# First attention of a four-layer sequence model: deeper step order, shared key projection, transposes by VectorE, tiles closed by pairs

## The chip, the cores and the metric

The kernel runs on one core of one Trainium2 chip. The time is the device time of one execution in microseconds (us). The core has five engines that each work through their own list of instructions: TensorE (PE in the profile; its weight loads are PEld), VectorE (DVE), ScalarE (ACT), GpSimd (POOL) and SyncE (SP). SP only issues transfers (DMAs) here. The engines meet through semaphores. SBUF is the working memory with 128 partitions; PSUM, 8 banks of 128 x 512 float32, takes what TensorE computes. [...]

## The reference

Eight stages follow one another on a sequence of 1024 tokens with 256 features: four times attention and a feed-forward part, each added to its input and followed by a layer normalization. The change is in the first attention and at the seam to the first feed-forward part, a mixture of eight experts of which each token takes two. Cut to what matters:

```python
# first attention: 16 query heads, 4 key/value heads, head size 128, window 64
q, k = rotate(x @ Wq), rotate(x @ Wk); v = x @ Wv
q1, q2 = q[..., :64], q[..., 64:]; k1, k2 = k[..., :64], k[..., 64:]
allowed = (col <= row) & (col >= row - 63)
a1 = softmax(where(allowed, q1 @ k1.T / 8, -inf))
a2 = softmax(where(allowed, q2 @ k2.T / 8, -inf))
diff = relu(a1 - lam[head] * a2)
diff = diff / (diff.sum(-1) + 1e-6)
x = layernorm(x + (diff @ v) @ Wo)

# first feed-forward part
logits = x @ Wr                        # 8 experts
top2, selected = top_k(logits, 2); w = softmax(top2)
out = sum over the two experts of w * ((clip(silu(x @ Wg)) * (x @ Wu)) @ Wd)
x = layernorm(x + out)
```

## The kernel before

The activations x lie in SBUF as eight tiles of 128 tokens (`k.x`), with a transposed copy `k.xT` made by `transpose_two` (two tiles at a time). Each stage is a function; `four_layers` calls them in turn, with a pool of buffers for each kind of tile, whose number stands in `SCOPES`.

**Units.** The first attention, `attn0`, works in 32 units: for each of the four key heads g, eight tiles t of 128 tokens. A unit takes the four query heads of g for its tile, as two pairs r and two blocks b of 64 queries, each with a window of 128 keys. Each head's vector is split into two halves f (first and second softmax).

**Operands.** Keys and queries are projected and rotated by `operands(g, half)` for 512 tokens at once, in steps that are spread over the units before they are needed: `next(ahead)` does one step. A step is a projection into a bank (`project`, L159) and a multiplication by cosine and sine (L627 for queries, L629 for keys, on VectorE); every second step adds the two rotating combinations on GpSimd (L634, L635). There are three pairs of steps per half: one for keys and two for queries. The key weights hold each head's columns twice, so that a key tile carries the same 64 rows in its lower and in its upper partitions, one copy for each pair r of query heads.

**A unit's steps.** `attn0_probs` writes the masks and the scores into two banks (L723, L733), takes the maxima of the eight rows of scores (L741, VectorE) and the exponentials (L749, ScalarE, eight instructions). Its second part makes the factor lam times the ratio of the two sums (L757, L758, L759) and, for each of four blocks, the difference (L765, VectorE) and its positive part with its sum (L769, ScalarE). Its third part takes the reciprocal of the sum (L773, L775) and multiplies by it on GpSimd (L777). `attn0_values` transposes the four blocks on TensorE (L786), copies them from PSUM on ScalarE (L788), multiplies by the values (L792), copies the result (L798), multiplies by the output weights (L804) and adds to x (`add_rows`, L240).

**The order.** `k.in_order()` makes TensorE, ScalarE, VectorE and GpSimd work in the order in which the program writes the instructions. SP is not among them: its order is set by the scheduler of the framework. The loop in `attn0` runs over i. In iteration i it writes, in this order: the transposes of unit i-3; the third part's predecessor for unit i-1 (factor and differences); a step of `operands` (and, for g = 0, the values of one tile, L166, L667); the values of unit i-3; the scores and exponentials of unit i; in odd iterations another step; the third part of unit i-1; the output sums of unit i-3. From scores to sums it is thus three iterations. The buffers limit how far an engine can run ahead: four banks, two double banks ("wide") for scores, three e, four diff, three pt and three ot tiles.

**The seam.** After the loop `k.layernorm()` normalizes four tiles at a time (L209, L210, the root on ScalarE at L227, L213). `ffn0` then stores the normalized rows to `moe_rows` in memory (L838), loads 24 pieces of expert weights (L844, L847), computes the router's logits for all eight tiles (L166), and finds the two largest and their indices (L874 to L880). From L881 to L956 it ranks the choices and builds the table of tokens for each block of an expert; `gather` (L233) then fetches the rows of `moe_rows` in that order.

## Time and profile before

| | us |
|---|---|
| median of three runs | 2273.65 |
| lowest and highest run | 2271.97, 2276.45 |
| the profiled execution | 2268.97 |
| its span, first to last instruction | 2267.1 |
| busy in the span: TensorE | 2073.2 |
| VectorE | 1284.3 |
| ScalarE | 872.9 |
| GpSimd | 528.9 |

The first attention lies in the first 292 us of the span. The last addition of its output (L240) ends at 291.75, and the first gather of the feed-forward part starts at 313.45. Two instructions that it has no use for yet stand later in the profile: VectorE's transposition of 32 x 32 squares (L402) and the transfers pt<-turned (L408), by which the second and the fourth attention transpose their probabilities.

How to read the lines that follow: a line of the busy times by stretch gives the stretch in us from the span's start, its length, then for each engine the busy time and the number of instructions, then the clock that TensorE was granted (1.00 is full), the share of the 16 DMA engines, and GB/s. A line of the groups gives line, engine, operation, output and inputs with their shapes and the count, then the busy time and the mean in ns, then the idle time ahead of them and what ended it. A line of the timeline gives start and duration in us. A line of the transfers gives the issues, the size of one and the median time from issue to landing in us.

### The profile page before, as it was taken

The page shows a single profiled execution, that of the slowest core. Times are in us where ns is not written, and L with a number is a line of the kernel's source. Part 1 is how long each engine was busy: PE and PEld are TensorE (multiplying, and loading weights), DVE is VectorE, ACT ScalarE, POOL GpSimd, SP SyncE. Part 2 cuts the span into 40 slices and gives each one's busy share as a digit, 9 for nine tenths or more (in the row PEclk, how much of TensorE's full clock was granted, in tenths as well). Part 3 has the DMA queues.
Part 4 walks back from the last instruction along what each step waited for, and adds up shares of the span by engine and source line. Part 5 has one row for each costly group of instructions (what it writes and reads, how often), then busy time and mean ns, then how long its engine had stood idle before and what let it go on. Part 6 is the DMA issues. An engine that isn't in the chain of part 4 may idle for free.

```text
span 2267.1 us, 24836 instructions
## 1 busy us (share of the span) xinstructions
PE 2073.2 (91%) x8127; PEld 1221.8 (54%) x8127; DVE 1284.3 (57%) x2599; ACT 872.9 (39%) x2268; POOL 528.9 (23%) x807
## 2 busy tenths in 40 slices
PE   7999769699999998988888998899999988999997
PEld 4666545466666665754444443366666665444443
DVE  5677646577776665455773445267777664222223
ACT  3666624343343433344454222654444442111111
POOL 4333221333333333321111000333333330000000
PEclk9999979799999999999999999999999999999999
DMA  4100054254545544013200000034344340111100
GB/s 161 36 10 29 29 174 117 62 140 112 135 108 132 155 112 100 10 56 111 68 1 10 28 28 2 19 85 110 90 115 90 77 113 19 38 31 53 31 1 19
DMA packets 124255, 159.60 MB, mean 70 GB/s; under 512 B 28928, under 2 KB 96064, under 8 KB 124128
## 3 DMA queue, kind: packets, MB, share of 16 engines
q1 hardware_dynamic: 114544, 132.98, 22.5%
q0 software_dynamic: 9584, 25.05, 3.7%
q8 instruction: 65, 1.06, 0.2%
q14 instruction: 62, 0.51, 0.1%
HBM read 68.72 MB, written 17.17 MB: 38 GB/s over the span
## 4 chain that ended last, share of the span: by engine, by line
PE 70%; DVE 13%; ACT 6%; DMA 4%; issue 3%; POOL 2%; SPq 2%; DVEq 0%; ACTq 0%; POOLq 0%
PE bank L159 23%; PE wide L274 8%; PE bank L439 8%; PE wide L307 8%; PE bank L166 4%; ACT e L749 3%; DMA pt<-turned 3%; DVE turned L402 2%; PE bank L1164 2%; PE bank L815 2%; PE bank L1601 1%; DVE st L741 1%; PE bank L995 1%; PE bank L1339 1%; POOL p L267 1%
## 5 line engine op out<-in xcount | busy, mean ns | idle before, releaser
L159 PE MATMUL bank<-xT,w 128*128 128x512 f32 (+2 forms) x1520 | 659.2, 567 | 4.0 <-DVE xT L185 3.8
L159 PEld LDWEIGHTS bank<-xT,w 128*128 128x128 f32 (+1 forms) x1520 | 288.6, 195 | 272.8 <-issue 251.3
L402 DVE STREAM_TRANSPOSE turned<-p 128x128 f32<-128x128 f32 (+7 forms) x232 | 283.6, 1223 | 84.2 <-DMA pt<-turned 48.2
L274 PE MATMUL wide<-k,q 128*128 128x512 f32 (+3 forms) x768 | 294.3, 493 | 18.4 <-ACT p L259 17.5
L267 POOL TENSOR_SCALAR p<-p,st 128x128 f32<-128x128 f32 (+7 forms) x256 | 190.3, 744 | 484.9 <-DVE st L266 484.3
L439 PE MATMUL bank<-pt,v 128*128 128x256 f32 x1216 | 282.6, 374 | 12.8 <-DMA pt<-turned 12.0
L439 PEld LDWEIGHTS bank<-pt,v 128*128 128x128 f32 x1216 | 227.5, 192 | 66.8 <-issue 24.1
L254 DVE TENSOR_REDUCE st<-wide 128x1 f32<-128x128 f32 (+7 forms) x256 | 193.4, 756 | 51.5 <-PE wide L279 44.4
L274 PEld LDWEIGHTS wide<-k,q 128*128 128x128 f32 x768 | 140.1, 192 | 135.3 <-issue 92.7
L307 PE MATMUL wide<-t,w 128*128 128x512 f32 x392 | 187.6, 601 | 8.2 <-DVE t L1878 4.8
L259 ACT ACTIVATE p<-wide,st,factor 128x128 f32<-128x128 f32 (+7 forms) x128 | 106.3, 830 | 214.0 <-POOL st L256 209.4
L259 ACT ACTIVATE p<-wide,st 128x128 f32<-128x128 f32 (+7 forms) x128 | 94.8, 740 | 237.2 <-DVE st L254 218.7
L2201 DVE TENSOR_TENSOR t<-t,bank 128x512 f32<-128x512 f32 x66 | 45.3, 687 | 247.2 <-PE bank L159 247.2
L2200 ACT ACTIVATE t<-bank 128x512 f32<-128x512 f32 x66 | 39.4, 597 | 294.1 <-PE bank L159 279.7
L307 PEld LDWEIGHTS wide<-t,w 128*128 128x128 f32 x392 | 68.2, 189 | 113.4 <-issue 48.3
L166 PE MATMUL bank<-w,xT 128*128 128x512 f32 (+3 forms) x320 | 123.9, 524 | 1.1 <-DVE st L266 0.8
L249 DVE TENSOR_TENSOR wide<-wide,causal 128x128 f32<-128x128 f32 x192 | 55.9, 291 | 97.7 <-PE wide L274 96.4
L749 ACT ACTIVATE e<-wide,st 128x128 f32<-128x128 f32 x256 | 89.8, 376 | 49.5 <-DVE st L741 34.4
L1626 ACT ACTIVATE pt<-wide 128x1024 f32<-128x1024 f32 (+3 forms) x96 | 75.6, 810 | 70.2 <-PE wide L1620 68.3
L2194 POOL COPY t<-select 99x128 bf16<-99x128 bf16 (+1 forms) x33 | 9.4, 291 | 318.7 <-PE bank L1045 318.7
L166 PEld LDWEIGHTS bank<-w,xT 128*128 128x128 f32 x320 | 58.8, 207 | 46.1 <-issue 39.9
L240 DVE TENSOR_TENSOR x<-bank,x 128x256 f32<-128x256 f32 x120 | 47.9, 409 | 55.5 <-PE bank L804 20.8
(317 smaller groups left out, 2921.3 us busy)
## 6 DMA issues: line engine op xcount, KB each, us to landing
pt<-turned SPq DMA_DIRECT2D x60, 240.0 KB, 4.8
pt<-turned SPq DMA_DIRECT2D x60, 176.0 KB, 3.5
w<-in_L_ffn_gate_up_dram SPq DMA_DIRECT2D x16, 512.0 KB, 3.7
pt<-turned SPq DMA_DIRECT2D x28, 256.0 KB, 4.9
pt<-turned SPq DMA_DIRECT2D x60, 112.0 KB, 2.6
pt<-turned SPq DMA_DIRECT2D x28, 224.0 KB, 4.3
w<-in_L_attn_Wq_dram SPq DMA_DIRECT2D x12, 512.0 KB, 9.7
w<-in_L_attn_Wo_dram SPq DMA_DIRECT2D x12, 512.0 KB, 3.8
```

Source lines behind the costliest of these rows:

```text
L159: self.nc.tensor.matmul(out, lhsT=weight(c), rhs=self.xcols(c, lo, n), start=c == 0, stop=c == NC - 1)
L166: self.nc.tensor.matmul(out, lhsT=self.xcols(c, lo, n), rhs=weight(c), start=c == 0, stop=c == NC - 1)
L249: nc.vector.tensor_tensor(scores[:, n - P : n], scores[:, n - P : n], self.causal, ALU.add)
L254: nc.vector.tensor_reduce(top, scores[:, :n], axis=AX.X, op=ALU.max, negate=True)
L259: nc.scalar.activation(probs[:, :n], scores[:, :n], AF.Exp, bias=top, scale=1.0 if scale is None else scale, accum_out=total,)
L267: self.nc.gpsimd.tensor_scalar(probs[:, :n], probs[:, :n], total, 1.0, ALU.mult, ALU.mult)
L274: self.nc.tensor.matmul(s[:, lo : lo + m], lhsT=query, rhs=key(lo, m), start=True, stop=not masked or lo + m < n, skip_group_check=masked,)
L307: nc.tensor.matmul(acc[m][:, half * HALF : (half + 1) * HALF], lhsT=down[:, m * P : (m + 1) * P], rhs=h, start=i == 0, stop=i == count - 1,)
L402: k.nc.vector.transpose(squares.rearrange("p b (k q) -> p b k q", q=32), probs[:, :n].rearrange("p (k i b) -> p b k i", b=4, i=32),)
L439: self.k.nc.tensor.matmul(out.rearrange("p (a q) -> p a q", q=32) if first else out.rearrange("p (s a q) -> p s a q", s=2, q=32), lhsT=val ...
L749: nc.scalar.activation(e[:, r, f, b, :], sc[:, r, f, b, :], AF.Exp, bias=top[:, at : at + 1], accum_out=total[:, at : at + 1],)
L1626: nc.scalar.activation(two[:, :, lo:], sc[:, :, lo:], AF.Exp)
```

## The change

- **Keys.** The columns of the key weights are no longer doubled; the half vectors of two neighbouring heads g and g+1 (g even) stand in one projection of 128 columns, one head in the lower and one in the upper 64 partitions. `operands` makes keys only for an even g, for both heads. GpSimd writes each head's half into its own tile on 64 partitions (four operations instead of two), and four transfers on SP copy each half into the other 64 partitions. There are six key tiles instead of four.
- **Transposes.** `attn0_turned` transposes 32 x 32 squares of the four blocks on VectorE (128 x 512 in one instruction), and four transfers of 32 partitions each put the squares into place in pt. TensorE's transposes and ScalarE's copy go. The values are multiplied by the same numbers in another arrangement of the free dimension.
- **Order.** In iteration i: the turn of unit i-3; a step of `operands` (and values for g = 0); scores and exponentials of unit i; factor and differences of i-1; the third part of i-2; the multiplication by the values for i-4; in odd iterations another step; the output sums of i-5. The loop has 37 iterations instead of 35.
- **Closing.** When both tiles of a pair have their last sum (g = 3), `close` is started for the pair: statistics, root (by a power on GpSimd, `power`), normalization and a store to `moe_rows`, the transposes, the router's logits with the maxima and indices of the pair, one part at a time, at two places in an iteration. What is left when the loop ends runs after it. `ffn0` finds the choices (`k.chosen`), the differences of logits (`k.prob`) and `k.xT` ready; `k.layernorm()`, the four calls of `transpose_two` ahead of `ffn0` and its router are gone.
- **Routing.** The comparison of columns (L931, 128 x 2048) is done in four parts, each ahead of the four products that use it; the copy of the tokens stands after the experts.

The router's weights `wr` move from the pool of weights to the constants and are loaded at the start. The helpers `add_stats`, `power`, `norm_tile`, `transpose_two` and `project_rows` are not changed.

```diff
--- before.py
+++ after.py
@@ -580,13 +580,7 @@
...
-    load_keys(0)
+    wk = k.weights([P, NC, 512], a["L0_attn_Wk"].rearrange("(c p) f -> p c f", p=P))
...
@@ -631,34 +624,96 @@
             if i == 0:
                 yield
         x, y = parts
-        nc.gpsimd.tensor_tensor(first, x[:, 0], y[:, 1], ALU.subtract)
-        nc.gpsimd.tensor_tensor(second, y[:, 0], x[:, 1], ALU.add)
+        for rows, out in first:
+            nc.gpsimd.tensor_tensor(out, x[rows, 0], y[rows, 1], ALU.subtract)
+        for rows, out in second:
+            nc.gpsimd.tensor_tensor(out, y[rows, 0], x[rows, 1], ALU.add)
         yield
 
...
+        heads = range(g, g + 2) if g % 2 == 0 else ()
         if half == 0:
-            keys[g] = [k.tile("k", [P, PAD + T]) for _ in range(2)]
-            for kt in keys[g]:
-                nc.gpsimd.memset(kt[:, :PAD], 0.0)
-        cols = slice(PAD + half * HALF, PAD + (half + 1) * HALF)
-        yield from rotated(
-            lambda i, c: wk[g // 2][:, c, (g % 2 * 2 + i) * P : (g % 2 * 2 + i + 1) * P],
-            half, *(kt[:, cols].rearrange("p (b n) -> p b n", n=64) for kt in keys[g]), 0.125,
-        )
+            for j in heads:
+                keys[j] = [k.tile("k", [P, PAD + T]) for _ in range(2)]
+                for kt in keys[j]:
+                    nc.gpsimd.memset(kt[:, :PAD], 0.0)
+        if heads:
+            cols = slice(PAD + half * HALF, PAD + (half + 1) * HALF)
+            own = [slice(j * 64, j * 64 + 64) for j in range(2)]
+            yield from rotated(
+                lambda i, c: wk[:, c, (g + i) * P : (g + i + 1) * P], half,
+                *(
+                    [
+                        (own[j], keys[g + j][f][own[j], cols].rearrange("p (b n) -> p b n", n=64))
+                        for j in range(2)
+                    ]
+                    for f in range(2)
+                ),
+                0.125,
+            )
+            for j in range(2):
+                for f in range(2):
+                    kt = keys[g + j][f]
+                    nc.sync.dma_start(out=kt[own[1 - j], cols], in_=kt[own[j], cols])
...
+                half, *([(slice(0, P), q[:, :, pair, :])] for q in queries[g, half]), 1.0,
...
+
+    wr = k.tile("const", [P, NC, 8], tag="wr")
+    nc.sync.dma_start(out=wr, in_=a["L0_ffn_Wr"].rearrange("(c p) e -> p c e", p=P))
+    k.moe_rows = k.tile("dram", [T, D], tag="moe_rows")
+    k.chosen = k.tile("const", [P, 2, NT], tag="chosen")
+    k.prob = k.tile("const", [P, 2, NT], tag="prob")
+
+    def close(t):
+
+
+        stats = k.tile("st", [P, 4, 2], tag="stats", bufs=2)
+        for i in range(2):
+            k.add_stats(t + i, stats)
+        rstd = k.power(stats[:, t % 4 : t % 4 + 2, 1], 2, LN_EPS, tag="root")
+        yield
+        for i in range(2):
+            k.norm_tile(t + i, stats, rstd[:, i : i + 1])
+        nc.sync.dma_start(
+            out=k.moe_rows[t * P : (t + 2) * P, :].rearrange("(t p) d -> p t d", p=P),
+            in_=k.x[:, t : t + 2, :],
+        )
+        yield
+        k.transpose_two(t)
+        yield
+        ps = k.bank()[:, :16].rearrange("p (t e) -> p t e", t=2)
+        for i in range(2):
+            k.project_rows(ps[:, i, :], lambda c: wr[:, c, :], (t + i) * P)
+        logits, top = (k.tile("st", [P, 2, 8]) for _ in range(2))
+        which = k.tile("st", [P, 2, 8], U32)
+        nc.vector.tensor_copy(logits, ps)
+        for i in range(2):
+            nc.vector.max(top[:, i, :], logits[:, i, :])
+            nc.vector.max_index(which[:, i, :], top[:, i, :], logits[:, i, :])
+        for i in range(2):
+            nc.vector.tensor_copy(k.chosen[:, i, t : t + 2], which[:, :, i])
+        nc.vector.tensor_tensor(
+            k.prob[:, 1, t : t + 2], top[:, :, 1], top[:, :, 0], ALU.subtract
+        )
+        yield
+
+    closing = []
+
+    def close_on():
+        if closing and next(closing[0], k) is k:
+            closing.pop(0)
 
...
@@ -679,15 +734,11 @@
         for _ in operands(*runs[0]):
             pass
         units = [(g, t) for g in range(4) for t in range(NT)]
-        ahead, made = iter(()), {}
-        for i in range(len(units) + 3):
-            ending = iter(())
-            if i >= 3:
-                g, t = units[i - 3]
-                ending = attn0_values(k, t, g, made.pop(i - 3), (even, odd), wo[g])
-            next(ending, None)
-            if i - 1 in made:
-                next(made[i - 1])
+        ahead, made, outputs = iter(()), {}, {}
+        for i in range(len(units) + 5):
+
+            if i - 3 in made:
+                made[i - 3] = attn0_turned(k, made[i - 3])
             if i < len(units):
                 g, t = units[i]
                 if t % 4 == 0:
@@ -700,16 +751,26 @@
                 next(ahead, None)
                 if g == 0:
                     make_values(t)
-            next(ending, None)
-            if i < len(units):
                 made[i] = attn0_probs(k, t, g, queries[g, t // 4], keys[g], lam)
                 next(made[i])
-                if i % 2:
-                    next(ahead, None)
+            close_on()
             if i - 1 in made:
-                made[i - 1] = next(made[i - 1])
-            for _ in ending:
+                next(made[i - 1])
+            if i - 2 in made:
+                made[i - 2] = next(made[i - 2])
+            if i - 4 in made:
+                g, t = units[i - 4]
+                outputs[i - 4] = attn0_values(k, t, g, made.pop(i - 4), (even, odd), wo[g])
+                next(outputs[i - 4])
+            if i % 2:
+                next(ahead, None)
+            close_on()
+            for _ in outputs.pop(i - 5, ()):
                 pass
+            if i >= 5 and units[i - 5][0] == 3 and units[i - 5][1] % 2:
+                closing.append(close(units[i - 5][1] - 1))
+        while closing:
+            close_on()
 
 
 def attn0_probs(k, t, g, queries, keys, lam):
@@ -778,21 +839,32 @@
     yield four
 
 
-def attn0_values(k, t, g, four, values, wo):
+def attn0_turned(k, four):
+
+
+
+    turned = k.tile("turned", [P, 4, P])
+    k.nc.vector.transpose(
+        turned.rearrange("p b (k q) -> p b k q", q=32),
+        four.rearrange("p k (i b) -> p b k i", b=4),
+    )
+    pt = k.tile("pt", [P, 4, 2, 2, 32])
+    for at in range(4):
+        k.nc.sync.dma_start(
+            out=pt[:, at].rearrange("p r b q -> p (r b q)"), in_=turned[at * 32 : at * 32 + 32]
+        )
+    return pt
+
+
+def attn0_values(k, t, g, pt, values, wo):
 
     nc = k.nc
-    ps = k.bank()
-    for i in range(4):
-        nc.tensor.transpose(ps[:, i * P : (i + 1) * P], four[:, i, :], k.ident)
-    pt = k.tile("pt", [P, 2, 2, P])
-    nc.scalar.copy(pt.rearrange("p r b n -> p (r b n)"), ps)
-    yield
     out = k.bank()
     for b in range(2):
         nc.tensor.matmul(
-            out[:, b * 256 : (b + 1) * 256].rearrange("p (r n) -> p r n", r=2),
-            lhsT=values[b][t][:, g * P : (g + 1) * P], rhs=pt[:, :, b, :],
-            start=True, stop=True,
+            out[:, b * 256 : (b + 1) * 256].rearrange("p (r a q) -> p r a q", r=2, a=4),
+            lhsT=values[b][t][:, g * P : (g + 1) * P],
+            rhs=pt[:, :, :, b, :].rearrange("p a r q -> p r a q"), start=True, stop=True,
         )
...
@@ -828,17 +900,11 @@
...
-    rows = k.tile("dram", [T, D], tag="moe_rows")
+    rows = k.moe_rows
     results = k.tile("dram", [blocks * P, D], tag="moe_results")
-    wr = k.weights([P, NC, 8], a["L0_ffn_Wr"].rearrange("(c p) e -> p c e", p=P))
...
-    for half in range(2):
-        nc.sync.dma_start(
-            out=rows[half * HALF : (half + 1) * HALF, :].rearrange("(t p) d -> p t d", p=P),
-            in_=k.x[:, 4 * half : 4 * half + 4, :],
-        )
...
@@ -866,21 +932,10 @@
...
-    ps = k.bank()[:, : NT * 8].rearrange("p (t e) -> p t e", t=NT)
-    for t in range(NT):
-        k.project_rows(ps[:, t, :], lambda c: wr[:, c, :], t * P)
-    logits, top = small([P, NT, 8]), small([P, NT, 8])
-    which = small([P, NT, 8], U32)
-    nc.vector.tensor_copy(logits, ps)
-    for t in range(NT):
-        nc.vector.max(top[:, t, :], logits[:, t, :])
-        nc.vector.max_index(which[:, t, :], top[:, t, :], logits[:, t, :])
-    chosen, mine = small([P, 2, NT]), k.tile("route", [P, 2, NT, 8], tag="mine", bufs=1)
-    for i in range(2):
-        nc.vector.tensor_copy(chosen[:, i, :], which[:, :, i])
...
@@ -928,10 +983,6 @@
...
-    nc.vector.tensor_tensor(
-        is_column, cols.unsqueeze(1).to_broadcast([P, 2 * NT, P]),
-        column.unsqueeze(2).to_broadcast([P, 2 * NT, P]), ALU.is_equal,
-    )
...
@@ -946,14 +997,15 @@
...
     for i in range(2 * NT):
+        if i % 4 == 0:
+            nc.vector.tensor_tensor(
+                is_column[:, i : i + 4, :], cols.unsqueeze(1).to_broadcast([P, 4, P]),
+                column[:, i : i + 4].unsqueeze(2).to_broadcast([P, 4, P]), ALU.is_equal,
+            )
         nc.tensor.matmul(
             ps, lhsT=is_column[:, i, :], rhs=is_block[:, i // NT, i % NT],
             start=i == 0, stop=i == 2 * NT - 1,
         )
-    low = small([P, blocks])
-    nc.vector.tensor_copy(low, ps[:, 0, :])
-    tokens = k.tile("route", [P, blocks], I32, tag="tokens", bufs=1)
-    nc.vector.scalar_tensor_tensor(tokens, ps[:, 1, :], float(P), low, ALU.mult, ALU.add)
...
@@ -964,10 +1016,13 @@
...
+    low = small([P, blocks])
+    nc.vector.tensor_copy(low, ps[:, 0, :])
+    tokens = k.tile("route", [P, blocks], I32, tag="tokens", bufs=1)
+    nc.vector.scalar_tensor_tensor(tokens, ps[:, 1, :], float(P), low, ALU.mult, ALU.add)
+
+    prob = k.prob
     p1, p2 = prob[:, 0, :], prob[:, 1, :]
-    nc.vector.tensor_tensor(p2, top[:, :, 1], top[:, :, 0], ALU.subtract)
...
@@ -2207,7 +2262,7 @@
...
-    attn0: dict(wide=2, mask=1, rope=1, k=4, v=16, q=4, t=4, e=3, diff=4, pt=3, ot=3),
+    attn0: dict(wide=2, mask=1, rope=1, k=6, v=16, q=4, t=4, e=3, diff=4, turned=2, pt=3, ot=3),
...
@@ -2226,11 +2281,11 @@
...
-            mine = {attn1: (), ffn1: (), ffn2: (), attn2: (0, 2), ffn3: ()}
+            mine = {ffn0: (), attn1: (), ffn1: (), ffn2: (), attn2: (0, 2), ffn3: ()}
             for t in mine.get(stage, range(0, NT, 2)):
                 k.transpose_two(t)
             stage(k, a)
-            if stage in (attn0, attn1):
+            if stage == attn1:
...
@@ -2256,11 +2311,10 @@
...
-    wk = a["L0_attn_Wk"].reshape(D, 4, 2, 1, 64)
-    a["L0_attn_Wk"] = np.broadcast_to(wk, (D, 4, 2, 2, 64)).reshape(D, 1024)
+    wk = a["L0_attn_Wk"].reshape(D, 2, 2, 2, 64)
+    a["L0_attn_Wk"] = wk.transpose(0, 1, 3, 2, 4).reshape(D, 512)
...
```

## The prediction

> **What bounds the kernel now.** I read the busy time by stage first, cutting at the starts of the score maxima (L741, one per unit: unit 0 at 28.26 us, 8 at 93.15, 28 at 247.44, 31 at 269.58).
>
> ```profile
> core 0: us, PE busy (x) PEld busy (x) DVE busy (x) ACT busy (x) POOL busy (x), PEclk, DMA share, GB/s
> 28.30:93.10 64.80, 60.76 (x308) 36.50 (x308) 44.57 (x95) 42.60 (x211) 22.27 (x21) 1.00 0.15 38
> 93.10:247.40 154.30, 141.86 (x796) 94.32 (x796) 116.27 (x250) 101.84 (x516) 58.31 (x54) 1.00 0.08 26
> 247.40:269.60 22.20, 15.13 (x103) 11.82 (x103) 10.66 (x35) 16.54 (x85) 3.12 (x3) 0.96 0.05 15
> 269.60:291.80 22.20, 15.61 (x63) 11.68 (x64) 9.79 (x36) 8.93 (x32) 3.18 (x8) 0.89 0.16 51
> 291.80:313.50 21.70, 9.50 (x69) 8.88 (x67) 14.10 (x71) 3.07 (x4) 0.05 (x1) 0.58 0.91 288
> ```
>
> In the loop (first two rows) TensorE is busy 92 to 94% at full clock: it is the bound. A unit takes 154.3/20 = 7.72 us. In the third row, with no projections left, no engine is full; the chain of waits there runs maxima, exponentials, copy to pt, values, scores. Row four is the drain, row five normalization and routing up to the first gather. Next the groups of instructions by line, for the second row alone:
>
> ```profile
> L159 PE MATMUL bank<-xT,w 128*128 128x512 f32 x116 | 55.6, 602 | 0.0
> L741 DVE TENSOR_REDUCE st<-wide 128x8 f32<-128x1024 f32 x20 | 24.4, 1221 | 3.0 <-PE wide L733 2.9
> L765 DVE SCALAR_TENSOR_TENSOR diff<-e,st 128x128 f32<-128x128 f32 x80 | 22.8, 347 | 1.4 <-DVE st L759 0.5
> L777 POOL TENSOR_TENSOR diff<-diff,st 128x512 f32<-128x512 f32 x20 | 20.8, 1040 | 27.0 <-DVE st L775 27.0
> L786 PE MATMUL bank<-ident,diff 128*128 128x128 f32 x80 | 12.0, 273 | 0.0
> L758 DVE TENSOR_TENSOR st<-st 128x4 f32<-128x4 f32 x20 | 8.9, 446 | 0.7
> ```
>
> L758 handles four numbers and averages 446 ns, though one alone takes 160. The timeline shows why:
>
> ```profile
> 181.90 1.26 POOL L635 TENSOR_TENSOR q<-t,t 128x512 f32<-128x512 f32 x1
> 181.92 1.26 DVE L758 TENSOR_TENSOR st<-st 128x4 f32<-128x4 f32 x1
> 183.12 1.03 POOL L777 TENSOR_TENSOR diff<-diff,st 128x512 f32<-128x512 f32 x1
> 183.21 0.96 DVE L759 TENSOR_TENSOR st<-st,lam 128x4 f32<-128x4 f32 x1
> ```
>
> Each small VectorE instruction ends just as the GpSimd one beside it ends. VectorE has slack today, so this costs little. Last, what the new instructions cost: the groups by form, first attention's later cousin (L402), and the list of transfers; then routing in the timeline.
>
> ```profile
> L402 DVE STREAM_TRANSPOSE turned<-p 128x512 f32<-128x512 f32 x15 | 16.6, 1110 | 0.2
> ```
> ```profile
> pt<-turned SPq DMA_DIRECT2D x28, 64.0 KB, 2.2
> ```
> ```profile
> 291.33 0.42 DVE L240 TENSOR_TENSOR x<-bank,x 128x256 f32<-128x256 f32 x1 [3.92 <-PE bank L804]
> 301.97 0.23 DVE L874 COPY route<-bank 128x64 f32<-128x64 f32 x1 [2.95 <-PE bank L166]
> 304.42 0.29 DVE L881 TENSOR_TENSOR mine<-cols,route 128x128 f32<-128x128 f32 x1
> 313.45 1.25 POOL L233 DMA_INDIRECT rows<-moe_rows,tokens  x1 [33.29 <-DVE experts L966]
> ```
>
> **What the Trainium skill says.** GPSIMD Engine Reference, Key points: GpSimd shares its SBUF interfaces with VectorE and contends with VectorE instructions that have two SBUF inputs. The trace agrees (1.26 us for L758). L765 has two SBUF inputs as well, but never met GpSimd here. VectorE: DVE Perf Modes, The three transpose paths: VectorE transposes only 32x32 blocks; so the four transfers per unit are needed to move the squares between partitions. TensorE: Matmul & The Clock Gate, Part 1: the clock halves after about 3.4 us of idling; here it is 1.00 in the loop and 0.89 in the drain.
>
> **The change, part by part.** TensorE, back to back: a projection 1.72 us, masks and scores 1.28, values 0.86, output sums 1.71, transposes 0.57. A four-unit stretch with six projections is 28.0 today. Keys of two heads at once leave six projections in the stretches that prepare an even g and four in the others: 8 projections fewer. Without transposes TensorE needs 25.7 or 22.3 per stretch, 6.4 or 5.6 a unit. ScalarE loses L788 (0.61): about 4.8 a unit.
>
> VectorE becomes the bound. Its new order in an iteration is: turn (1.05 from start to next start), rotation (1.13), maxima (1.14), the factors (0.60), four L765 (1.06), norm (0.37), second rotation in odd iterations, add (0.38). Today's trace gives all these steps; the turn is L402's 1.11, less the overlap of about 0.06 that the rotations show. Iteration by iteration:
>
> - One rotation: the turn of unit u follows the norm of u by only an add, and needs L777 of u: 0.17 to start, 1.04, 0.08 back. So VectorE idles: 1.05+1.13+1.14+0.60+1.06+0.37+1.29 = 6.64. Behind the waiting turn stand the next rotation and maxima; ScalarE's exponentials wait for the maxima, and TensorE for the banks that the rotation frees.
> - Two rotations: the second covers L777: 6.9. No rotation: 5.5.
> - A rotation pair that ends in the first rotation sends GpSimd 2 operations (queries, 2x1.27) or 4 (keys: two heads by two parts, each 64 partitions; I price each at 1.27, since its free size is the same). They run while the factors and L765 want SBUF. The maxima cover one; the rest hold VectorE: about 1.2 us for queries, 3.4 for keys, if L765 is held too (2.3 if it is not, 0 to 1 if 64 partitions cost half). I take the dear values, since the skill's sentence covers L765 and today's holds last to the end of each operation; the cheap ones go into rival (a).
>
> Six-projection stretch: 6.64 + (6.9+3.4) + (6.64+1.2) + 6.9 = 31.7. Four-projection stretch: 6.64 + (6.9+1.2) + (6.64+1.2) + 5.5 = 28.1. Today: 31.1 in both.
>
> Units 8 to 28 are three stretches of four projections and two of six: 147.7 against 154.3, **-6.6**.
> Units 0 to 8, today limited by TensorE: two projections fewer (-3.4), five transposes (-2.9), two output sums and one values put off by the depth (-4.3): **-10.6**. VectorE, with few stages filled, needs no more than the 54.2 that are left. The start stays: the key copies come off GpSimd at about 20 us and land by about 23, and the queries release the first scores at 26.28 anyway. They hold the SP queue ahead of weights that are wanted only units later.
> Units 28 to 31: three iterations of 5.5 against 22.1: **-5.6**.
> Drain. From the last maxima: exponentials 2.9, factors and L765 in the next iteration, norm, L777, turn; adding VectorE's steps, with the first pairs' closings among them (statistics 1.4, norms 0.75, copy 0.68, maxima and indices 1.6 a pair), iterations 31 to 34 take 6.0+5.8+3.3 and the last turn 1.05: 16.2. Then 4 issues at 0.6, 2.2 to land, values 0.9, two output sums 3.4 and the add 0.4: 9.3 (the copy to ot goes under the first sum). Together 25.5 against 22.2. Expert weights (256 KB each, 5.4 to 5.9 us to land) stand ahead of the last two units' transfers on SP: +0.7, at most +8. So **+4**.
> After the last add, two of the four pairs of tiles are closed, the third is halfway. Its transposes, rows and maxima take 4.3; the fourth's statistics 1.4, root 0.5, norms 0.8, transposes and copy 1.3, rows 1.6, maxima and indices 1.6: 11.5 to the comparison at L881, today 12.7 from the add's end (304.42-291.75). Splitting the column comparison by fours lets TensorE start early: -0.4 of 9.0. **-1.6**. Gathers wait also for the last moe_rows transfer, which may queue behind 2 MB of weights (about 7 us at 288 GB/s), less than the routing's 8.6.
>
> Other edits cost nothing: wr and the key weights (512 KB less) load early; the roots move from ScalarE to GpSimd, which is idle by then; six k buffers only hold memory. In the loop the 128 transfers of squares take SP 2.4 us an iteration and need 4.6 from the turn, while values come an iteration later: covered by 6 us, and without that cover TensorE would wait up to 4.6 per unit. In the built order, weight loads for the second attention stand between them on SP; those wait for projections or output sums that end before the next turn.
>
> Sum: -6.6-10.6-5.6+4-1.6 = -20.4. The profiled execution took 2268.97 (span 2267.1) and becomes 2248.6; the median of the runs is 4.7 higher: 2273.65-20.4 = **2253**.
>
> **Rivals.** (a) *TensorE stays the bound*: GpSimd's short operations hold nothing, and the turn finds L777 done. Then units 8 to 28 take 3x22.3+2x25.7 = 118.3, not 147.7: 2224, and half of that gain 2238. For it: the hold on L765 was never seen. Against: L758 shows the hold, and the turn follows its norm at once. (b) *The turn eats the loop's gain*: VectorE is also held in the turn, or key operations of 64 partitions are dearer, at 0.5 us a unit: +10, and a drain that meets the weights fully +5: 2268. For it: GpSimd is at work 58 of 154 us. Against: L402 keeps 1110 ns beside GpSimd's L267. (c) *Slower: the clock*. TensorE, now waiting on VectorE up to 3.4 us in key iterations, loses full clock. Units 8 to 28 need 5.9 a unit of TensorE work; the change turns slower once that exceeds 8.4 us, a mean clock below 0.70; at 0.65 it is 9.1 a unit, 2288. For it: 0.89 in the drain. Against: units 28 to 31 ran 0.96 at 68% busy, and the loop would be at 80%.
>
> **How the numbers follow.** Forecast 0.55 (2243 to 2263), (a) 0.17, (b) 0.16, (c) 0.12. The range leaves out most of (c) and the far end of (a): 2232 to 2270. Differences below 0.2% (4.5 us) can't be told from none by such runs: faster takes the forecast, (a) and over half of (b), 0.81; same 0.08; slower 0.11.
>
> **What would show it.** In the changed profile: VectorE at about 90% in units 8 to 28 and TensorE at 80%; idle before the turns put down to GpSimd's multiply (L838), near 0.8 us in half the iterations; L819 and L820 averaging over 500 ns and L826 stretched in key iterations; stretches of about 28 and 32 us; the first gather near 293. The prediction is wrong if TensorE waits for pt, if the clock leaves 1.00 in the loop, or if the turn never waits.

## The result and the profile after

The changed kernel takes 2255.48 us (median of four runs, 2252.74 to 2258.68) where the kernel before took 2272.81 us beside it (2271.30 to 2276.45): ratio 0.9922, 95% interval 0.9909 to 0.9935. The forecast was 2253. The profiled execution has a span of 2253.0 us against 2267.1.

The busy times by stretch, cut where the maxima of units 0, 8, 28 and 31 start (L802, formerly L741) and at the last addition and the first gather (us from the start, length; busy time and count of each engine; TensorE's clock; DMA share; GB/s):

```profile
core 0: us, PE busy (x) PEld busy (x) DVE busy (x) ACT busy (x) POOL busy (x), PEclk, DMA share, GB/s
28.40:85.20 56.80, 53.60 (x257) 31.08 (x258) 43.73 (x90) 36.73 (x195) 21.26 (x18) 0.94 0.41 99
85.20:230.20 145.00, 129.20 (x693) 85.99 (x691) 127.03 (x265) 90.64 (x500) 56.16 (x52) 0.95 0.26 63
230.20:246.40 16.20, 12.88 (x90) 9.54 (x90) 12.99 (x38) 13.59 (x76) 3.12 (x3) 1.00 0.23 51
246.40:276.00 29.60, 22.61 (x93) 18.41 (x92) 20.20 (x75) 8.39 (x38) 6.37 (x12) 0.83 0.63 183
276.00:296.20 20.20, 6.25 (x48) 4.72 (x46) 13.32 (x64) 1.49 (x2) 0.71 (x2) 0.56 0.57 181
```

The loop's main part (second row) went from 154.3 to 145.0 us; VectorE is busy 88% of it. The drain (fourth row) went from 22.2 to 29.6 us, at a clock of 0.83. The first gather comes at 296.18 us instead of 313.45: 17.3 us, as much as the medians differ.

Groups of the changed kernel in that second row (busy us, mean ns of one, idle time before and who ended it):

```profile
L826 DVE SCALAR_TENSOR_TENSOR diff<-e,st 128x128 f32<-128x128 f32 x80 | 27.1, 400 | 0.7
L847 DVE STREAM_TRANSPOSE turned<-diff 128x512 f32<-128x512 f32 x20 | 22.0, 1102 | 10.8 <-POOL diff L838 10.8
L820 DVE TENSOR_TENSOR st<-st,lam 128x4 f32<-128x4 f32 x20 | 12.3, 616 | 0.7
L628 POOL TENSOR_TENSOR k<-t,t 64x512 f32<-64x512 f32 x4 | 5.0, 1262 | 4.9 <-DVE t L622 4.7
```

The turn costs 1102 ns, and VectorE stands still ahead of it for 10.8 us in 12 of 20 units until GpSimd's multiplication (L838) is done. GpSimd's operations on 64 partitions take 1262 ns, as long as those on 128. The timeline of one pair of key steps shows what they hold:

```profile
151.42 2.60 POOL L628 TENSOR_TENSOR k<-t,t 64x512 f32<-64x512 f32 x2 [2.35 <-DVE t L622]
152.78 1.26 DVE L820 TENSOR_TENSOR st<-st,lam 128x4 f32<-128x4 f32 x1
154.08 3.27 DVE L826 SCALAR_TENSOR_TENSOR diff<-e,st 128x128 f32<-128x128 f32 x4
154.08 2.60 POOL L630 TENSOR_TENSOR k<-t,t 64x512 f32<-64x512 f32 x2
```

L820, 0.16 us alone, takes 1.26; the four L826, 1.14 us together elsewhere, take 3.27: 3.2 us per key pair, where the prediction's dear value was 3.4.

### The profile page after: what moved, and what is told of

Its sections match the earlier page's. It is cut to its first block, busy times and chain, and to the rows that moved or that the text cites. A ratio compares the mean times of both kernels' runs of the same rounds, so it can differ in the third digit from the quotient of the medians.

```text
span 2253.0 us, 24727 instructions
## 1 busy us (share of the span) xinstructions
PE 2060.1 (91%) x7967; PEld 1211.3 (54%) x7967; DVE 1306.5 (58%) x2640; ACT 851.0 (38%) x2232; POOL 532.1 (24%) x811
## 3 DMA queue, kind: packets, MB, share of 16 engines
q8 instruction: 64, 1.05, 0.2%
## 4 chain that ended last, share of the span: by engine, by line
PE 66%; DVE 9%; ACT 3%; DMA 3%; issue 3%; POOL 2%; SPq 1%; DVEq 0%; ACTq 0%; POOLq 0%
PE bank L159 22%; PE wide L274 9%; PE bank L439 8%; PE wide L307 8%; PE bank L166 4%; DVE turned L402 2%; PE bank L1219 2%; DMA pt<-turned 2%; PE bank L887 2%; PE bank L1656 2%; PE bank L1394 1%; PE bank L1050 1%; ACT pt L1681 1%; PE wide L1669 1%; POOL p L267 1%
## 5 line engine op out<-in xcount | busy, mean ns | idle before, releaser
L159 PE MATMUL bank<-xT,w 128*128 128x512 f32 (+1 forms) x1488 | 644.9, 567 | 6.3 <-DVE xT L185 6.0
L159 PEld LDWEIGHTS bank<-xT,w 128*128 128x128 f32 x1488 | 286.5, 196 | 272.9 <-issue 248.0
L166 PE MATMUL bank<-w,xT 128*128 128x512 f32 (+2 forms) x288 | 118.6, 549 | 0.8 <-DVE st L266 0.8
L249 DVE TENSOR_TENSOR wide<-wide,causal 128x128 f32<-128x128 f32 x192 | 55.8, 291 | 97.1 <-PE wide L274 96.0
L166 PEld LDWEIGHTS bank<-w,xT 128*128 128x128 f32 x288 | 52.6, 196 | 46.2 <-issue 40.0
L1633 DVE TENSOR_REDUCE st<-wide 128x2 f32<-128x1024 f32 x64 | 64.3, 1020 | 21.2 <-PE wide L1629 10.3
```

The source lines that it names most:

```text
L159: self.nc.tensor.matmul(out, lhsT=weight(c), rhs=self.xcols(c, lo, n), start=c == 0, stop=c == NC - 1)
L166: self.nc.tensor.matmul(out, lhsT=self.xcols(c, lo, n), rhs=weight(c), start=c == 0, stop=c == NC - 1)
L1633: nc.vector.tensor_reduce(st[:, i, :] if half else to, sc[:, :, :n], axis=AX.X, op=ALU.max, negate=True,)
```

## The experiments

All twelve runs in one table, with the kernel before and the changed one. Stages are read from the traces: us between the maxima of the units named, then from the last maxima to the end of the last addition (drain), and from there to the first gather (seam). Ratios are to the kernel before, measured on the same chip (2272.28 us beside e1 to e4, 2278.56 beside e5 to e8, 2274.17 beside e9 to e12). Medians from different chips therefore compare less well than ratios.

| run | units 0-8 | 8-28 | 28-31 | drain | seam | first gather | median | ratio, 95% interval |
|---|---|---|---|---|---|---|---|---|
| before | 64.9 | 154.3 | 22.1 | 22.2 | 21.7 | 313.5 | 2272.81 | 1 |
| changed | 56.8 | 145.0 | 16.2 | 29.7 | 20.2 | 296.2 | 2255.48 | 0.9922, 0.9909-0.9935 |
| e12, changed again | 55.6 | 144.1 | 16.2 | 29.7 | 20.2 | 294.4 | 2251.08 | 0.9901, 0.9874-0.9928 |
| e1, keys per head | 56.5 | 149.2 | 16.7 | 29.1 | 20.2 | 301.1 | 2260.85 | 0.9942, 0.9920-0.9965 |
| e2, TensorE transposes of i-3 | 75.2 | 179.6 | 19.2 | 25.0 | 20.2 | 347.8 | 2298.90 | 1.0114, 1.0088-1.0140 |
| e3, before + shared keys | 63.9 | 153.6 | 23.7 | 22.7 | 20.8 | 313.0 | 2270.56 | 0.9989, 0.9974-1.0004 |
| e4, turn after maxima | 54.8 | 140.3 | 15.2 | 28.4 | 20.2 | 287.4 | 2242.64 | 0.9878, 0.9851-0.9904 |
| e5, TensorE transposes of i-4 | 53.3 | 150.1 | 15.9 | 26.3 | 21.0 | 294.1 | 2252.32 | 0.9882, 0.9863-0.9902 |
| e6, before + depth | 55.8 | 146.0 | 15.9 | 23.5 | 21.7 | 291.1 | 2249.69 | 0.9869, 0.9853-0.9886 |
| e7, no closing | 58.6 | 144.1 | 16.2 | 23.8 | 19.9 | 290.1 | 2253.05 | 0.9882, 0.9865-0.9898 |
| e8, e4 + values last | 53.9 | 133.9 | 14.5 | 29.7 | 19.9 | 280.0 | 2241.81 | 0.9830, 0.9814-0.9847 |
| e9, e8 + no closing | 57.0 | 134.1 | 14.5 | 23.4 | 19.9 | 277.5 | 2239.53 | 0.9848, 0.9824-0.9872 |
| e10, e9 + two key operations | 51.8 | 129.7 | 14.5 | 23.4 | 20.4 | 267.6 | 2230.59 | 0.9801, 0.9775-0.9828 |
| e11, e10 + early last step | 50.6 | 129.0 | 16.0 | 23.4 | 21.3 | 268.1 | 2233.28 | 0.9814, 0.9785-0.9842 |

What follows the first gather is the same code in all of them, and yet takes 1951 (e4) to 1965 us (e11) in the profiles. Differences of a few us in the medians are therefore read together with the stages. The stages vary too: units 0 to 8 took 53.9 and 57.0 us in e8 and e9, whose code is the same up to there, and 55.6, 56.8 and 58.6 in e12, the changed kernel and e7; the seam with its old code took 19.9 to 21.7 in seven runs.

### Which part brings the gain: e1, e3, e6, e2, e5

**Keys per head again (e1).** `operands` and the key weights of the kernel before, all else as changed:

```diff
-        heads = range(g, g + 2) if g % 2 == 0 else ()
+        keys[g] = [k.tile("k", [P, PAD + T]) for _ in range(2)]
...
+            lambda i, c: wk[g // 2][:, c, (g % 2 * 2 + i) * P : (g % 2 * 2 + i + 1) * P],
```

> The changed kernel with the keys projected head by head again; depth, turn and closing stay. Theory (VectorE is the bound of the loop): TensorE gets its eight projections back, but in units 8 to 28 nothing is lost: each four-unit stretch then has three pairs of rotations of the cheap kind, 1.05 us per turn, two GpSimd operations per pair, 31.7 - (3.4 - 1.2) = 29.5 us, five of them 147.5 against the 145.0 measured. Only units 0 to 8, where TensorE leads, lose 2 x 1.72 = 3.4 us. Time: 2255.5 + 2.5 + 3.4, about 2261 (2256 to 2264). Rival (TensorE is still the bound and the saved projections are the gain): all eight projections come back, 13.8 us, 2269.

Measured 2260.85: the eight projections are worth 5.4 us by the medians (the intervals overlap) and 4.2 us in units 8 to 28, not 13.8. Stretches of four units take 29.3 to 30.8 us, near the 29.5 worked out. That fits the theory that VectorE sets the loop's pace. That units 0 to 8 would lose 3.4 us did not come (56.5 against 56.8).

**Shared keys alone (e3).** The same edit the other way round, on the kernel before.

> The kernel before with nothing but the keys of two heads at once. There TensorE is the bound of units 0 to 28, so each of the eight projections left out is worth its 1.72 us: 2272.8 - 13.8 = 2259 (2255 to 2263), unless GpSimd's four key operations hold VectorE by 3.4 us in two stretches and VectorE has no slack for it there, 2263. Rival (keys are worth nothing because something other than TensorE sets the pace): 2272.

No gain: 0.9989, and units 0 to 28 are 1.6 us shorter where eight projections of 1.72 us were left out. GpSimd's key operations hide no gain: of the five stretches in units 8 to 28, the three that lost two projections each and have no key operations are only 0.2, 1.1 and 0.7 us shorter, and the two with key operations are 0.7 and 0.6 longer. The theory of this run fell, and with it the reading at the head of the prediction: TensorE did not set the pace of the kernel before. What VectorE waited for in the kernel before, in units 8 to 28 (us in total, times, longest):

```profile
DVE st L757 <- ACT e L749: 19.6, 19, 1.8
```

With the eight projections gone, in e3, this wait grew to 23.4 us. One unit of the kernel before in the timeline:

```profile
155.32 1.22 DVE L741 TENSOR_REDUCE st<-wide 128x8 f32<-128x1024 f32 x1
156.63 0.37 ACT L749 ACTIVATE e<-wide,st 128x128 f32<-128x128 f32 x1 [1.31 <-DVE st L773]
159.56 0.18 DVE L757 RECIPROCAL st<-st 128x4 f32<-128x4 f32 x1 [1.73 <-ACT e L749]
160.16 1.14 DVE L765 SCALAR_TENSOR_TENSOR diff<-e,st 128x128 f32<-128x128 f32 x4
161.22 1.22 DVE L629 SCALAR_TENSOR_TENSOR t<-bank,rope 128x1024 f32<-128x1024 f32 x1
162.45 1.23 DVE L741 TENSOR_REDUCE st<-wide 128x8 f32<-128x1024 f32 x1
```

Maxima of a unit, its eight exponentials, its factors and differences, the rotation, the maxima of the next unit: in the old order the factors of unit i-1 stood ahead of the maxima of unit i, so that this chain closed once per unit, 7.13 us here. From the start of the maxima to the first factor it takes 4.23 to 4.53 us in every one of the twenty units. The four units of a stretch mostly take 7.13, 7.87, 7.14 and 8.94 us. In the second, VectorE also waits 0.66 us for scores from TensorE (2.9 us in all twenty units); in the fourth, GpSimd holds two of the factors (1.26 and 0.96 us in the lines of the prediction). TensorE's 92% were the work that fitted into that time.

**The depth alone (e6).** The kernel before with the new order and nothing else:

```diff
-        for i in range(len(units) + 3):
+        for i in range(len(units) + 5):
+            if i - 4 in made:
+                g, t = units[i - 4]
+                outputs[i - 4] = attn0_values(k, t, g, made.pop(i - 4), (even, odd), wo[g])
+                next(outputs[i - 4])
...
+            if i - 1 in made:
+                next(made[i - 1])
+            if i - 2 in made:
+                made[i - 2] = next(made[i - 2])
+            if i - 4 in outputs:
+                next(outputs[i - 4])
+            if i % 2:
+                next(ahead, None)
+            for _ in outputs.pop(i - 5, ()):
+                pass
```

> The kernel before with nothing but the deeper order: transposes and copy of unit i-4, projection, scores and maxima of i, factors and differences of i-1, norm and multiplication of i-2, values of i-4, second projection, output sums of i-5. Keys per head, transposes on TensorE, no closing. Theory (in the order before, exponentials stand between the maxima of one unit and the factors that VectorE needs ahead of the next maxima, and this chain of about 7.5 us per unit, not TensorE, sets the pace; the depth takes it apart): units 8 to 28 fall from 154.3 to what TensorE needs, 140 to 146 us, units 0 to 8 by 4 to 7, units 28 to 31 by 6, the drain gains 1 to 3 us: 2248 to 2256. Rival (TensorE was the bound, and the depth by itself is worth nothing in the loop): 2266 or more.

Measured 2249.69, ratio 0.9869: the depth alone is worth the whole change, and by the intervals somewhat more than the changed kernel's first measurement; the second (e12) overlaps it. Two stages missed what was expected of them: units 0 to 8 gained 9.1 us, and the drain lost 1.3 instead of gaining 1 to 3. VectorE's waits in units 8 to 28:

```profile
DVE t L629 <- PE bank L159: 16.3, 10, 1.8
DVE t L627 <- PE bank L159: 11.0, 10, 1.7
```

No wait for exponentials is left; VectorE now waits for projections. The same 145 us of the kernel before and then of e6:

```profile
85.00:230.00 145.00, 133.62 (x739) 88.60 (x738) 109.64 (x235) 95.99 (x486) 54.77 (x51) 1.00 0.07 23
```
```profile
85.00:230.00 145.00, 140.17 (x794) 94.58 (x793) 111.36 (x250) 100.31 (x520) 58.50 (x54) 1.00 0.09 26
```

TensorE's products cover 97% of it instead of 92%.

**TensorE's transposes in the deep order (e2, e5).** Both put TensorE's four transposes and ScalarE's copy in place of the turn; e2 for unit i-3, where the turn stands, e5 for unit i-4:

```diff
-            if i - 3 in made:
-                made[i - 3] = attn0_turned(k, made[i - 3])
+            if i - 4 in made:
+                made[i - 4] = attn0_turned(k, made[i - 4])
...
-    k.nc.vector.transpose(
+    ps = k.bank()
+    for i in range(4):
+        k.nc.tensor.transpose(ps[:, i * P : (i + 1) * P], four[:, i, :], k.ident)
```

> The changed kernel with TensorE's four transposes and ScalarE's copy in place of the turn and its transfers, at the same place in the order (unit i-3 at the head of iteration i); shared keys, depth and closing stay. Theory (the turn and its wait for GpSimd made VectorE the bound): VectorE gets back 1.05 us and the wait per unit and needs 25.6 us in a six-projection stretch, TensorE 28.0 and 24.6 us, so TensorE is the bound again: units 8 to 28 take 2 x 28.0 + 3 x 24.6 = 130 us instead of 145.0, up to 138 if its waits of before come back; units 0 to 8 lose five transposes, 2.9 us; the drain is 4 us shorter without transfers. Time 2239 (2238 to 2249), faster than the changed kernel. Rival (taking the transposes off TensorE is what gained): 32 x 0.57 = 18 us are lost, 2270 or more.

Measured 2298.90, slower than the kernel before. The number lies where the rival had it, 2270 or more, but the rival's reason, 18 us of transposes, does not explain 43 us over the changed kernel. The timeline of e2 shows a chain that closes within one iteration:

```profile
213.96 1.04 POOL L838 TENSOR_TENSOR diff<-diff,st 128x512 f32<-128x512 f32 x1 [8.34 <-DVE st L836]
215.05 0.66 PE L848 MATMUL bank<-ident,diff 128*128 128x128 f32 x4
215.55 1.88 PE L159 MATMUL bank<-xT,w 128*128 128x512 f32 x4
217.59 1.05 PE L794 MATMUL wide<-k,q 64*128 64x128 f32 x16
218.70 1.23 DVE L802 TENSOR_REDUCE st<-wide 128x8 f32<-128x1024 f32 x1
220.43 1.14 DVE L826 SCALAR_TENSOR_TENSOR diff<-e,st 128x128 f32<-128x128 f32 x4
221.68 0.18 DVE L836 RECIPROCAL st<-st 128x4 f32<-128x4 f32 x1
222.03 1.04 POOL L838 TENSOR_TENSOR diff<-diff,st 128x512 f32<-128x512 f32 x1 [4.55 <-DVE st L836]
```

Multiplication to multiplication is 8.07 us, each step behind the other, because an in-order TensorE that waits for unit i-3's multiplication holds the projection and scores of unit i behind it. The chain through the turn runs on VectorE and leaves out TensorE's transposes, projection and scores: there the wait ahead of the turn is 0.9 us. For e5:

> The changed kernel with TensorE's transposes and ScalarE's copy in place of the turn, but of unit i-4 at the head of iteration i, so that they follow GpSimd's multiplication of the same unit by a whole iteration; the values of i-4 follow later in the same iteration. In the run with the transposes of i-3 the chain multiplication, transposes, projection, scores, maxima, factors, differences, norm, multiplication closed on itself once per iteration, 8.1 us. Theory (that chain, and not the transposes' price, made that run slow; without it TensorE is the bound with 28.0 and 24.6 us per stretch): units 8 to 28 take 130 to 138 us against 145.0, time 2240 to 2250. Rival (VectorE's turn is the better place whatever the order): 2262 or more.

The time is just above the upper end (2252.32), the reason holds only in part: without the chain the transposes are as good as the turn by the medians, but units 8 to 28 take 150.1 us, not 130 to 138. In its key iterations TensorE stands and then runs slowly:

```profile
123.74 3.64 PE L159 MATMUL bank<-xT,w 128*128 128x512 f32 x4 [2.23 <-DVE t L620]
```

The rotation that frees the bank is late because the differences ahead of it are held by GpSimd's key operations (3.21 us there). With keys per head and no such operations, e6 needs 146.0. So under the depth the four combinations of keys and transposes take, in units 8 to 28: 146.0 (per head, TensorE), 150.1 (shared, TensorE), 149.2 (per head, turn), 145.0 (shared, turn). Either edit alone loses 3 to 4 us; the two together win 1, no more than the same code varies from run to run in this stage (145.0, 144.1 and 144.1 in the changed kernel, e12 and e7).

### Closing: e7

```diff
-            close_on()
...
-        while closing:
-            close_on()
...
-            if stage == attn1:
+            if stage in (attn0, attn1):
                 k.layernorm()
```

With it `ffn0` is that of the kernel before, router and whole column comparison included.

> The changed kernel without the closing by pairs and without the edits of routing: the seam of before stands behind the loop again (layer normalization, transposes, router of all eight tiles). Keys, turn and depth stay. The loop up to the last maxima does not change (246.3). Theory by the sum of the prediction: the drain loses the 4.4 us of closing that stand in VectorE's queue and the waits of its small matrix products, last add about 22 to 25 us after the last maxima instead of 29.6; then the seam of before, 21.7 us to the first gather instead of 20.2: first gather at 290 to 293 against 296.2, time 2250 to 2254. Rival (closing is what shortens the seam): first gather at 300 or later, 2260 or more.

First gather at 290.1, time 2253.05, as expected: closing lengthens drain and seam together by 6 us. It does not shorten the seam (20.2 with, 19.9 without) and lengthens the drain from 23.8 to 29.7. The drain of e7, to be laid beside the fourth row of the changed kernel above:

```profile
246.40:270.20 23.80, 15.91 (x72) 12.47 (x72) 15.61 (x51) 10.04 (x40) 4.33 (x9) 1.00 0.67 193
```

TensorE has 72 products there instead of 93 (those of closing are gone) and keeps its full clock; in the changed kernel it runs at 0.83. Two of the changed kernel's lines show what closing does to TensorE's order:

```profile
251.12 0.43 PE L178 MATMUL bank<-ident,x 128*128 128x128 f32 x1 [2.31 <-DVE x L213]
256.13 3.76 PE L876 MATMUL bank<-w,ot 128*128 128x256 f32 x8
```

TensorE stands at closing's transposes until VectorE has normalized the pair, with the values of the next unit behind them, and then runs at half clock from 251.3 to 261.3: the eight output products take 3.76 us, in e7 1.99. The clock is not the whole price. In e1 the drain, with closing, takes 29.1 us at 0.94. Nor do closing's products alone bring the low clock: with closing and TensorE's transposes (e2, e5) the drain keeps 1.00 and takes 25.0 and 26.3 us, against 23.5 in e6, which has neither closing nor turn. How much of the 6 us is waiting and how much is clock stays open.

The changed kernel's last addition also stands behind the third pair's normalization, which waits for the root on GpSimd:

```profile
274.19 0.71 POOL L221 TENSOR_TENSOR root<-root,minus_half 128x2 f32<-128x2 f32 x1 [9.35 <-DVE root L220]
274.93 0.73 DVE L213 TENSOR_SCALAR x<-x,stats,root 128x256 f32<-128x256 f32 x2 [0.83 <-POOL root L221]
275.58 0.42 DVE L240 TENSOR_TENSOR x<-bank,x 128x256 f32<-128x256 f32 x1
```

### The waits in the loop taken away: e4, e8, e9, e10, e11

**Turn after the maxima (e4).**

```diff
-            if i - 3 in made:
-                made[i - 3] = attn0_turned(k, made[i - 3])
...
                 next(made[i])
+            if i - 3 in made:
+                made[i - 3] = attn0_turned(k, made[i - 3])
             close_on()
```

> The changed kernel with one move: VectorE's turn of unit i-3 is written after the maxima of unit i instead of at the head of iteration i. Theory (the turn heads VectorE's queue before GpSimd's multiplication is done, and GpSimd's rotating combinations then hold the factors and differences): the wait of 0.9 us goes in the iterations that have one (10.8 us in units 8 to 28), and the turn, which is not held beside GpSimd, covers 1.1 us of the combinations; a six-projection stretch takes about 27.9 us and one of four 24.4 to 25, units 8 to 28 about 129 to 131 instead of 145.0, time 2240 (2236 to 2246). Rival 1 (the turn is held beside GpSimd as the other instructions are): only the waits go, 2245. Rival 2 (the transfers of the squares now land too late for the values, about 1 to 2 us per unit, with TensorE's whole order behind them): no gain, 2255 or more.

The time came (2242.64), the stage only in part: 140.3 us. VectorE no longer waits for the multiplication; instead, as rival 2 had it, TensorE waits for the squares (units 85 to 230 us):

```profile
PE bank L864 <- DMA pt<-turned: 13.5, 11, 2.9
```

**Values last (e8).** The block of unit i-4's values moves behind the output sums of i-5.

> The kernel with the turn after the maxima, and the values of unit i-4 written behind the output sums of i-5 instead of ahead of the second projection. In the run with the turn moved, TensorE waited 13.5 us in units 85 to 230 us for the transfers of the squares, at the values, with the second projection behind them, and VectorE then waited for that projection. Theory: with two to four microseconds more for the transfers these waits go, VectorE becomes the bound again at 28 and 24.4 us per stretch, units 8 to 28 take 129 to 133 us instead of 140.3, time 2234 (2230 to 2238). Rival (the loop of that run is held by something else, VectorE's holds or TensorE's clock): 2240 to 2245.

Units 8 to 28 fall to 133.9 us (first gather at 280.0), and TensorE has no wait for the squares in them: this was what held the loop of e4. The median, 2241.81, is 8 us above the expected one and lies where the rival had it, but the stage contradicts the rival. The kernel before took 5.8 us more beside this run than beside the changed kernel, so the ratios compare better: 0.9830 against 0.9922.

**Without closing (e9).**

> The kernel with the turn after the maxima and the values last, and without closing and routing edits. Theory (closing lengthens the drain by more than it takes from the seam, 6.1 us at the first gather in the changed order): first gather at 274 instead of 280.0, time 2236 (2232 to 2239). Rival (the cost of closing was one of the changed order, where VectorE had no slack, and is smaller here): 2240 or more.

Drain and seam take 43.4 instead of 49.6 us, 6.2 less: closing costs as much in this order as in the changed one. Units 0 to 8, whose code is the same, took 3.1 us more, so the first gather moves by 2.5 us only, to 277.5. The median, 2239.53, lies between the theory and the rival and decides nothing.

**Two key operations (e10).**

```diff
-                        (own[j], keys[g + j][f][own[j], cols].rearrange("p (b n) -> p b n", n=64))
-                        for j in range(2)
+                    [(slice(0, P), kt[:, cols].rearrange("p (b n) -> p b n", n=64))]
+                    for kt in both
...
-                    nc.sync.dma_start(out=kt[own[1 - j], cols], in_=kt[own[j], cols])
+                    nc.sync.dma_start(
+                        out=swap[f][64 - j * 64 : 128 - j * 64, cols],
+                        in_=both[f][j * 64 : j * 64 + 64, cols],
+                    )
```

> The kernel of the run just named, with one more edit: GpSimd writes both heads' halves together on 128 partitions into one tile (two operations per key pair instead of four of 64 partitions), four transfers make a second tile with the halves exchanged, and the heads read the two tiles crosswise. Theory (four operations of 1.26 us hold VectorE's factors and differences by 3.2 us per key pair, as the trace of the changed kernel shows): the two six-projection stretches fall from 29.4 and 30.3 us to about 28, units 0 to 8 and the start gain 1 to 3 us, in all 4 to 6 us: 2231 (2228 to 2234). Rival (TensorE covers the hold in those stretches): gain under 2 us, 2235.

2230.59, and units 8 to 28 at 129.7. The number is the expected one, but against e9 it is 8.9 us less instead of 4 to 6: 4.4 come in units 8 to 28, and 5.2 in units 0 to 8, where the same code differs by 3 us from run to run. Its groups in that stage show that the hold is gone (the differences are L775 here):

```profile
L775 DVE SCALAR_TENSOR_TENSOR diff<-e,st 128x128 f32<-128x128 f32 x80 | 22.8, 348 | 0.7
L630 POOL TENSOR_TENSOR k<-t,t 128x512 f32<-128x512 f32 x2 | 2.6, 1280 | 0.0
```

The mean of 400 ns is back at 348. With e11, which can't be told from it, this is the fastest version, ahead of both kernels: 2230.59 against 2251.08 for the changed kernel on the same chip.

**Early last step (e11).**

```diff
+            if i % 4 == 3:
+                next(ahead, None)
...
-            if i % 2:
+            if i % 4 == 1:
                 next(ahead, None)
```

> The kernel of the run just named, with the last step of operands of each half (the second step of iterations 3, 7, 11 and so on) written ahead of the factors instead of behind the norm, so that GpSimd makes the last queries ahead of its multiplication. Theory (at every change of the half TensorE waits up to 1.8 us, in the changed kernel up to 3.2 us, for queries that GpSimd makes behind its multiplication, and its clock then falls): waits of about 6 us and some time at the lower clock go: 2227 (2224 to 2231). Rival (the combinations then hold the factors and differences of the same iteration by 1 to 2 us, seven times): no gain or a loss, 2232 or more.

The waits for queries went (3.2 us in units 0 to 28 of e10, none in e11), but the time did not: 2233.28, no difference that can be told from e10. The rival's number came, and its hold is in the trace, though on the factors alone: in units 8 to 28 two of the factors average 328 and 265 ns instead of 210 and 162, 4.4 us in all, while the differences keep their 347. Units 0 to 28 gain 1.9 us all the same, and units 28 to 31, which the edit does not touch, lose 1.6; what kept the time where it was stays open.

**The change once more (e12).**

> The changed kernel once more, unchanged, beside the three others, since the deeper order alone had run on another chip than the changed kernel. Theory (the deeper order alone is worth at least the whole change): ratio to the kernel before near 0.992, above the 0.985 to 0.989 of the deeper order alone; stages within 0.5 us of the first profile. Rival (the two chips differ, and the change is as fast as its deeper order alone): ratio 0.987.

0.9901, between the two expectations, and its stages lie within 1.2 us of the first profile, not 0.5.

## Why the prediction was right, and where not

**The forecast held**: 2255.5 for 2253, direction and size. Step by step, with the second profile's value (e12) in brackets:

- *Units 8 to 28, -6.6.* Measured -9.3 (-10.2). The terms are right: turn 1.05 (1.10 from its group), wait 0.8 predicted and 0.9 measured, hold of the keys 3.4 and 3.2. Stretches of 31.7 and 28.1 us were worked out; 28.01, 31.55, 31.54 and 27.99 came. The fifth took 25.91: it ends with the maxima of unit 28, an iteration that has no rotation, and I had counted one with it. That is 1.1 of the 2.2 us; the rest is spread over the stretch's four iterations.
- *Units 28 to 31, -5.6.* Measured -5.9.
- *Units 0 to 8, -10.6.* Measured -8.1 (-9.3), and the terms are wrong. I took TensorE for the bound and counted two projections and five transposes as gains, and 4.3 us for the depth. With neither of the two, the depth alone gives -9.1. What was missed besides: at unit 4 TensorE waits for queries that GpSimd makes behind its multiplication, and runs slowly after it:

```profile
53.47 2.45 PE L794 MATMUL wide<-k,q 64*128 64x128 f32 x16 [3.20 <-POOL q L628]
56.00:63.80 7.80, 7.80 (x31) 4.37 (x32) 5.26 (x13) 5.11 (x26) 2.19 (x2) 0.74 0.29 64
```

  The scores take 2.45 us instead of 1.05, and the clock is 0.74 in the next unit.
- *Drain, +4.* Measured +7.5 (+7.5). The term that was mis-sized is closing: I added the work of its instructions to VectorE's queue, but not TensorE's stop at its transposes, not the half clock after it and not the last addition's place behind the third pair. Without closing the turn costs nothing here: 23.8 us with it and 23.5 with TensorE's transposes. With closing the turn does cost: 29.7 us against 26.3 (e5).
- *After the last addition, -1.6.* Measured -1.5. But e7 has the old seam and needs no longer, so this is not closing's gain.

The misses of -2.7, +2.5 and +3.5 cancel in part, and that is luck: sum -17.3 for -20.4.

**The step that failed** is the first one: "In the loop (first two rows) TensorE is busy 92 to 94% at full clock: it is the bound." The Trainium skill warns of this (Perfetto Trace Analysis, Identifying the Most-Contended Engine: the busy share of matmuls is not a good measure of how near TensorE is to its limit; the busy share of the weight loads is one of two that it names instead). The trace agrees: weight loads were busy 94.3 of 154.3 us, 61%. The chain through the exponentials was in the same trace, as VectorE's wait of nearly 1 us per unit. In units 8 to 28 the sum survived because it priced the new loop from VectorE's own steps and used only the old loop's measured length. Had it been used to choose among the parts, it would have chosen wrongly: it credits the keys and the transposes, and calls the depth a postponement.

**Rivals.** (a), TensorE stays the bound: no; the holds are there. (b), the turn is held by GpSimd: no, 1102 ns; in the changed kernel it seldom meets a GpSimd operation, but in e10 eleven turns do and take 1.10 to 1.12 us. (c), the clock: it did leave 1.00, against the forecast (0.94 and 0.95 in the first two rows), down to 0.75 in 99.3 to 113.2 us. It cost little: units 8 to 12, with that dip, took 28.01 us and without it, in e12, 27.04; units 12 to 16 took 31.55 us at full clock and, in e12, 31.53 at 0.95. Whether the 1 us of the first pair is the clock's or that of the wait ahead of it is not shown.

**Signs.** As forecast: VectorE near 90%, idle before 12 of 20 turns, L820 over 500 ns, L826 stretched in key iterations. Not so: L819 stays at 217 ns, the first gather comes at 296 instead of 293, TensorE is busy 89% instead of 80 (in part because its products are longer at the lower clock: e10 has as many, at 0.99, busy for 122.5 us against 129.2), and TensorE waits for pt, three times, 3.7 us in all. The prediction had named three signs of its being wrong. Two of them came, both small: the clock left 1.00 in the loop, and TensorE waited for pt.

## What to carry to other kernels

With engines that work in order, look for the chain that closes once per iteration before naming a busy engine the bound: for each wait that recurs in every unit, ask how many iterations lie between producer and consumer. Relieving the busiest engine gave nothing in the old order (e3), and by itself little in the deeper one (146.0 to 145.0 us in units 8 to 28). It paid when the waits that it brought were taken away: e8's 133.9 us are less than the 141.2 that TensorE was busy in the same units of e6. And an instruction at the head of a queue that waits for last iteration's result puts everything behind it into the chain: move it behind work that is ready, and move its consumer by as much. Work taken into a drain has to be counted with what engines that work in order wait for because of it, and not by its own instructions alone.

## What the runs showed of the hardware

- A transposition by VectorE (one SBUF input) beside a GpSimd operation takes its 1.1 us (e10: 1.10 to 1.12, eleven times), while the four differences (two SBUF inputs) are held, 3.27 us instead of 1.14. The Trainium skill (GPSIMD Engine Reference, Key points) names two SBUF inputs among what contends; both sides of that are seen here.
- GpSimd takes 1262 ns for 64 x 512 numbers and 1270 for 128 x 512 (L628 of the changed kernel): half the partitions save nothing.
- TensorE ran at half speed after shorter stops than the 3.4 us that the Trainium skill gives (TensorE: Matmul & The Clock Gate, Part 1): after 2.23 us in e5, where four products then took 3.64 us instead of 1.88. The measurement decides, but no threshold follows from it: in e7's drain it stopped for 2.26 us and the stage stayed at 1.00.
